# A four-layer graph network: GpSimd forms the bias of the layer norm, the heads' norm's last product gets a place in TensorE's order, and all places are chosen anew

## The chip, the cores and the metric

The kernel runs on one core of one Trainium2 chip. The metric is the device time of one execution in microseconds (us). The kernel before takes 3956.56 us, the median of 3 runs (3955.46 to 3960.7). The profiled execution spans 3957.2 us, with a mean granted TensorE clock of 0.973 of full speed.

A core has five engines with queues of their own: TensorE (PE: matrix products and transposes, with its weight loads PEld beside them), VectorE (DVE), ScalarE (ACT), GpSimd (POOL) and SyncE (SP, which issues the transfers here). They run side by side and wait for each other through semaphores.

## The reference

Thirty-two graphs (B) of 512 nodes (N) with 256 features (D) each go through four layers. Each layer is an attention over the edges of the graph, and is wrapped as `x = layernorm(x + layer(x))`.

```python
# layer 0: 4 heads of 64; e = leaky_relu(e_src + e_dst), masked softmax
out = relu(att @ h + bias) + h
out = (out - out.mean(-1)) / sqrt(out.var(-1) + 1e-6) * gamma + beta   # per head
# layer 1: 1 head; e = relu(f_src + f_dst), masked softmax, then elu
h = x @ W;  out = elu(softmax(where(adj > 0, e, NEG)) @ h)
# layer 2: 8 heads of 32, scaled dot products on adj | adj.T | eye
x1 = layernorm(x + softmax(where(allowed, q @ k.T / sqrt(32), -inf)) @ v @ Wo.T + bo, ln1)
out = layernorm(x1 + relu(x1 @ W1.T + b1) @ W2.T + b2, ln2)
# layer 3: 1 head; e = leaky_relu(f_i + f_j, 0.2), masked softmax
out = softmax(where(adj == 0, NEG, e)) @ (x @ W.T)
```

So a graph has six layer norms over all 256 features (one at the end of each layer, two within layer 2), and one norm per head of 64 in layer 0.

## The kernel before, in words

**Tiling.** The 512 nodes of a graph are four blocks (R = 4) of 128 partitions; a tile such as `y` is 128 x 4 x 256, so a row of the profile with 128x1024 is a whole graph's features. A product goes to one bank of PSUM (512 floats a partition), which `bank` hands out: two banks for layers 0 and 1 (stage "a"), four for the qkv, attention and projection stages ("b"), two for feed forward and layer 3 ("c"). A product must wait until the bank that it is to take has been read. PSUM tiles have the name of what they hold: `o` the products of masked weights with values, `s` the scores, `cp` the context of a head pair transposed, `ctp` its transposition back (and, with input `ctx`, the transposition of the divided context), `wop` the output projection, `f1p` and `f2p` the two products of the feed forward, `gp` a column spread along a row, `h0p`, `h1p`, `h3p` the projections of the layers, `xt1p`, `xt2p`, `xt3p` transpositions of a layer's input, `qkp` and `vp` queries and keys, and values.

**Order.** `graph(b)` is a generator that passes through all stages of one graph: edges, x, layer 0, layer 1, mask, qkv, attention, projection, feed forward, layer 3. Each `yield` in a stage is a cut; `paced` (line 108) turns the i-th cut of stage `name` of graph b into the key `PERIOD * b + PLACES[name][i]`, and `heapq.merge` (line 740) over all 32 generators emits the pieces in the order of their keys. Graphs so overlap as in a pipeline: while one is in its feed forward and layer 3, the next is in attention and the one after in layer 0 and 1. TensorE keeps the emitted order (`tc.manual_schedule` for PE alone, line 739); what the other engines run is ordered by the scheduler of the framework, from the data that each instruction waits for. Keys matter only by their order, so that a finer unit of `PERIOD` does nothing by itself. `in_place` (line 103) ties an instruction of another engine to TensorE's order: it makes the instruction wait for the latest product that was emitted before it. `mask` and `symmetric` use it for the conversion of the edges (line 362) and the union of the two masks (line 381).

**Layer norm** (lines 259 to 280). VectorE takes `bn_stats` and `bn_aggr` of each block of rows (lines 265, 266: mean and variance in `mv`), and forms variance + eps (line 268). GpSimd raises it to the power -0.5 (line 269: 128x4). VectorE multiplies mean, -1 and the power (line 270). ScalarE then computes `y * scale + bias` for the four blocks in place (line 274), where scale is the power and bias that product. `rs` has three rows: variance + eps, power, bias.

**Heads' norm** (lines 282 to 297), used in layer 0. VectorE subtracts the means, ScalarE squares, VectorE sums (line 295 is the sum / 64 + eps), GpSimd raises 128x16 elements to the power -0.5 (line 296), and VectorE multiplies the features by it (line 297). Line 438 (gamma) and 439, and a layer norm follow.

**Around them.** In attention, for each of four head pairs and each of four blocks of keys, TensorE computes the scores, ScalarE their exponentials `pr` (line 549), VectorE multiplies by the mask (line 551, 128x1024, two inputs from SBUF), and `cp` takes four of these as its input; ScalarE copies `cp` to `cs` (line 567). In the projection, VectorE takes reciprocals (line 582) and divides `ctp` into `ctx` (line 586). In layer 1, an `o` product is followed by a reciprocal (line 473, VectorE), relu and exp on ScalarE (474, 475) and two sums on VectorE (476, 478). In the feed forward, ScalarE makes `ft` of `f1p` (line 633), VectorE adds `f2p` (line 647), and lines 649 and 650 follow the second norm. In layer 0, line 398 adds the bias to the values and line 408 scales them (both 128x1024 from SBUF). In layer 3, line 660 is the exponential that `gp` is made from. In layers 0, 1 and 3, line 391 makes the masked weights `pt` (128x512), and line 344 copies `gp` to SBUF.

After all graphs, one flag is read; if a check on edges and sums had failed, a general version would compute everything (it isn't run here).

Of the kernel before, what the change touches and what calls it, by code (L numbers as in the profile page):

```python
# [14 lines left out]
ALU = mybir.AluOpType  # L15
# [7 lines left out]
F32R = mybir.dt.float32r  # L23


PERIOD = 1205
PLACES = {
    "edges": [-226, -113, -5, -1],
    "x": [84],
    "mask": [1464, 1488, 1689, 1689],  # L30
    "layer 0": [
        188, 232, 373, 373, 427, 532, 536, 536, 536, 549, 603, 603, 603, 630, 637, 712, 712, 728,
        758, 758, 766, 779, 787, 791,
    ],
    "layer 1": [1024, 1057, 1078, 1123, 1135, 1135, 1151, 1276, 1299, 1366, 1385],
    "qkv": [1656, 1721, 1771, 1771, 1771, 1849, 1893, 1903, 2016, 2028],
    "attention": [
        1976, 2013, 2122, 2148, 2174, 2174, 2174, 2178, 2178, 2217, 2277, 2277, 2278, 2333, 2363,
        2405, 2452, 2475, 2493, 2527,
    ],  # L40
    "projection": [2590, 2597, 2597, 2606, 2687, 2722, 2820, 2876, 2902, 2949],
    "feed forward": [
        3051, 3062, 3135, 3169, 3169, 3196, 3221, 3327, 3328, 3357, 3381, 3419, 3447, 3483, 3512,
        3560, 3618, 3683,
    ],
    "layer 3": [3958, 3998, 4038, 4074, 4074, 4074, 4082, 4179, 4182, 4185, 4185],
}
STAGES = {"edges": "a", "x": "a", "layer 0": "a", "layer 1": "a", "feed forward": "c", "layer 3": "c"}
ALL = mybir.DependencyInfo(mybir.DependencyClass.Sync, mybir.DependencyReason.DATA)
# [22 lines left out]
def fast_path(ctx: ExitStack, tc: tile.TileContext, a: dict, out: bass.AP, bad: bass.AP):  # L72
# [8 lines left out]
    nc = tc.nc  # L81
    B, N, D = a["x"].shape
    P = 128
    R = N // P
    K = D // P
    H, _, HO = a["w0"].shape
# [13 lines left out]
    def product(what, *args, **kwargs):  # L100
        latest[0] = what(*args, **kwargs).ins.name  # L101

    def in_place(op):

        if latest[0]:
            tc.add_manual_dep(op.ins, latest[0], ALL, reason="in its place")

    def paced(b, name, units):

        i = 0  # L110
        while True:
            stage[0] = STAGES.get(name, "b")
            try:
                next(units)
            except StopIteration as end:
                return end.value
            yield PERIOD * b + PLACES[name][i]
            i += 1
# [124 lines left out]
    def buf(shape, tag, name, bufs, dtype=F32):  # L243

        return sb.tile(shape, dtype, tag=tag + stage[0], name=name, bufs=bufs)

    def bank(name, dtype=F32):
        shape = [P, 2048 // (2 if dtype == BF16 else 4)]
        n = 4 if stage[0] == "b" else 2
        return ps.tile(shape, dtype, tag="mm" + stage[0], name=name, bufs=n)  # L250

    def part(name):

        return buf([P, N], "part", name, {"a": 7, "b": 6, "c": 5}[stage[0]])

    def all_rows(v):
        return v.unsqueeze(1).to_broadcast([P, R, D])

    def layernorm(y, eps):

        st = buf([P, R, 6], "bn", "bn", 2)
        mv = buf([P, R, 2], "mv", "mv", 2)
        rs = buf([P, 3, R], "rs", "rs", 2)
        for r in range(R):
            nc.vector.bn_stats(st[:, r, :], y[:, r, :])  # L265
            nc.vector.bn_aggr(mv[:, r, :], st[:, r, :])
        var = mv[:, :, 1]
        nc.vector.scalar_tensor_tensor(rs[:, 0, :], var, eps, var, op0=ALU.add, op1=ALU.max)  # L268
        nc.gpsimd.tensor_tensor(rs[:, 1, :], rs[:, 0, :], mhalf[:, :R], op=ALU.pow)  # L269
        nc.vector.scalar_tensor_tensor(  # L270
            rs[:, 2, :], mv[:, :, 0], -1.0, rs[:, 1, :], op0=ALU.mult, op1=ALU.mult
        )
        for r in range(R):
            nc.scalar.activation(  # L274
                y[:, r, :],
                y[:, r, :],
                AF.Identity,
                bias=rs[:, 2, r : r + 1],
                scale=rs[:, 1, r : r + 1],
            )  # L280

    def head_layernorm(y, eps):

        G = R * H
        yg = y.rearrange("p r (g d) -> p (r g) d", g=H)
        st = buf([P, 3, G], "lnh", "st", 2)
        nc.vector.tensor_reduce(st[:, 0, :], yg, axis=X, op=ALU.add)
        nc.vector.tensor_scalar_mul(st[:, 0, :], st[:, 0, :], 1.0 / HO)
        nc.vector.tensor_sub(yg, yg, st[:, 0, :].unsqueeze(2).to_broadcast([P, G, HO]))
        for i in range(2):  # L290
            g = slice(i * G // 2, (i + 1) * G // 2)
            sq = part("sq").rearrange("p (g d) -> p g d", d=HO)
            nc.scalar.activation(sq, yg[:, g, :], AF.Square)
            nc.vector.tensor_reduce(st[:, 1, g], sq, axis=X, op=ALU.add)
        nc.vector.tensor_scalar(st[:, 1, :], st[:, 1, :], 1.0 / HO, eps, op0=ALU.mult, op1=ALU.add)  # L295
        nc.gpsimd.tensor_tensor(st[:, 2, :], st[:, 1, :], mhalf[:, :G], op=ALU.pow)  # L296
        nc.vector.tensor_mul(yg, yg, st[:, 2, :].unsqueeze(2).to_broadcast([P, G, HO]))

    def evacuate(i, dst, src):
        if i % 2:  # L300
# [17 lines left out]
    def project(xt, w, cols, name):  # L318

        h = buf([P, R, cols], "h", name, {"a": 2}.get(stage[0], 1))  # L320
        for r in range(R):
            yield
            p = bank(name + "p")
            for k in range(K):
                product(nc.tensor.matmul,
                    p[:, :cols],
                    xt[:, k, r * P : (r + 1) * P],
                    w[:, k, :cols],
                    start=k == 0,
                    stop=k == K - 1,  # L330
                )
            nc.scalar.copy(h[:, r, :], p[:, :cols])
        return h

    def along(cols, name):

        yield
        p = bank("gp")
        for r in range(R):
            product(nc.tensor.transpose,  # L340
                    p[:, r * P : (r + 1) * P], cols[:, r, :].to_broadcast([P, P]), ident
            )
        g = buf([P, N], "gb", name, {"a": 2}.get(stage[0], 1))
        nc.scalar.copy(g, p)  # L344
        return g
# [42 lines left out]
    def kept(name, g, edges, f):  # L388

        t = part(name)  # L390
        nc.vector.scalar_tensor_tensor(t, g, f, edges, op0=ALU.max, op1=ALU.mult)  # L391
        return t


    def layer0(x, xt, at, rd):
        h = yield from project(xt, w0, D + 2 * H, "h0")
        values = hv[:, :, :, :HO]
        nc.vector.tensor_add(
            values,
            h[:, :, :D].rearrange("p r (h e) -> p r h e", h=H),  # L400
            bias0.rearrange("p (h e) -> p h e", h=H).unsqueeze(1).to_broadcast([P, R, H, HO]),
        )
        ex = buf([P, 2, H, R], "ex", "ex0", 2)
        s, d = h[:, :, D : D + H], h[:, :, D + H :]
        nc.scalar.activation(ex[:, 0], s.rearrange("p r h -> p h r"), AF.Exp, scale=-0.99)
        nc.scalar.activation(ex[:, 1], d.rearrange("p r h -> p h r"), AF.Exp, scale=0.99)
        nc.scalar.activation(hv[:, :, :, HO], d, AF.Exp, scale=0.01)
        nc.vector.tensor_mul(values, values, hv[:, :, :, HO:].to_broadcast([P, R, H, HO]))
        y = sb.tile([P, R, D], F32, tag="y", name="y0", bufs=3)
        for hh in range(H):  # L410
            gb = yield from along(ex[:, 0, hh, :].unsqueeze(2), "gb0")
            pt = [kept("pt0", gb, at[:, j, :], ex[:, 1, hh, j : j + 1]) for j in range(R)]
            p = bank("o0")
            o = p[:, : R * HC].rearrange("p (r c) -> p r c", r=R)
            for r in range(R):
                yield
                for j in range(R):
                    product(nc.tensor.matmul,
                    o[:, r, :],
                        pt[j][:, r * P : (r + 1) * P],  # L420
                        hv[:, j, hh, :],
                        start=j == 0,
                        stop=j == R - 1,
                    )
            rdh = rd[:, hh * R : (hh + 1) * R].unsqueeze(2)
            nc.vector.reciprocal(rdh, o[:, :, HO:])
            nc.vector.scalar_tensor_tensor(
                y[:, :, hh * HO : (hh + 1) * HO],
                o[:, :, :HO],
                0.0,  # L430
                rdh.to_broadcast([P, R, HO]),
                op0=ALU.max,
                op1=ALU.mult,
            )
        nc.vector.tensor_add(x, x, all_rows(bet0))
        nc.vector.tensor_add(y, y, h[:, :, :D])
        head_layernorm(y, 1e-6)
        nc.vector.tensor_mul(y, y, all_rows(gam0))
        nc.vector.tensor_add(y, y, x)
        layernorm(y, 1e-5)  # L440
        return y

# [275 lines left out]
    def graph(b):  # L718
        yield PERIOD * b + PLACES["edges"][0]
        rd = sb.tile([P, ND], F32, tag="rd", name="rd", bufs=3)  # L720
# [675 lines left out]
```

## Time and profile before

| what | value |
| --- | --- |
| time, median of 3 | 3956.56 us |
| TensorE busy | 94% of 3957.2 us, 18982 matmuls |
| VectorE busy | 72%, 5626 instructions |
| ScalarE busy | 49%, 4257 instructions |
| GpSimd busy | 9%, 266 instructions |
| power of the layer norm (line 269), 192 times | 1006 to 1991 ns, median 1009 |
| power of the heads' norm (line 296), 32 times | 2914 to 3812 ns, median 3807 |

The profile lists busy time by group of instructions, the waits (idle time of an engine before an instruction, with the instruction that ended the wait as its releaser), a timeline, and the granted TensorE clock. In a timeline row stand the start, the length, the engine, the line, the operation, output and inputs, shapes, how many instructions the row gathers, and in brackets the idle time before it with its releaser. All products of TensorE go through one helper, so they have line 101, and are told apart by the names of their tiles. TensorE's overlapping records make the busy time of a row somewhat longer than its share of the queue. A steady period, from one graph to the next, is a good unit to look at: between the first and the last graphs the same pattern recurs every 117 to 119 us.

### The profile page before, as it was taken

What the parts mean: (1) busy time and instruction counts of PE and PEld (TensorE: products, weight loads), DVE (VectorE), ACT (ScalarE), POOL (GpSimd) and SP (SyncE); (2) the same over time, 40 slices, a digit from 0 to 9 for tenths busy, and PEclk for the clock granted to TensorE, in tenths of its full rate; (3) what the DMA queues carried; (4) which work ended last, traced back from release to release, by engine and by line L of the source; (5) the groups of instructions that cost most, each with busy time, mean ns of one, the idle gap of its engine ahead of it and who ended that gap; (6) DMA issues with size and microseconds to landing.
All of it is one profiled execution on the core that took longest, in us unless ns stands there. A gap on an engine that the chain in (4) does not pass through costs nothing.

```text
span 3957.2 us, 53344 instructions
## 1 busy us (share of the span) xinstructions
PE 3722.2 (94%) x18982; PEld 2832.6 (72%) x18982; DVE 2830.4 (72%) x5626; ACT 1947.7 (49%) x4257; POOL 362.0 (9%) x266
## 2 busy tenths in 40 slices
PE   5899999999999999999999999999999999999996
PEld 4577777777777777777777777777777777777665
DVE  4667777777777777777777777777777777777753
ACT  2444455544455544455554455544455554555442
POOL 0000010010010101010101010101011101011000
PEclk6899999999999999999999999999999999999998
DMA  3222212222222222222222222222222222221110
GB/s 105 75 72 67 70 58 63 70 75 69 68 58 63 70 75 69 68 61 61 69 75 75 62 64 63 64 75 75 62 64 63 65 79 71 62 67 55 52 50 12
DMA packets 180433, 261.20 MB, mean 66 GB/s; under 512 B 36801, under 2 KB 72769, under 8 KB 180161
## 3 DMA queue, kind: packets, MB, share of 16 engines
q1 hardware_dynamic: 180160, 257.71, 23.0%
q8 instruction: 154, 2.52, 0.3%
q14 instruction: 119, 0.97, 0.1%
HBM read 106.57 MB, written 16.78 MB: 31 GB/s over the span
## 4 chain that ended last, share of the span: by engine, by line
PE 51%; DVE 17%; issue 10%; ACT 7%; POOL 7%; SPq 2%; DMA 1%; DVEq 0%; POOLq 0%; ACTq 0%
PE o L101 12%; PE f1p L101 7%; PE f2p L101 6%; DVE pr L551 5%; PE cp L101 4%; POOL rs L269 4%; PE qkp L101 3%; PE h3p L101 3%; POOL st L296 3%; PE wop L101 3%; PE h1p L101 3%; ACT y L274 2%; SPq L510 2%; DVE bn L265 2%; ACT pr L549 2%
## 5 line engine op out<-in xcount | busy, mean ns | idle before, releaser
L551 DVE TENSOR_TENSOR pr<-pr,a 128x1024 f32<-128x1024 f32 x512 | 616.7, 1216 | 220.4 <-ACT pr L549 220.2
L391 DVE SCALAR_TENSOR_TENSOR pt<-gb,ex,at 128x512 f32<-128x512 f32 x768 | 533.3, 743 | 136.3 <-ACT gb L344 136.3
L274 ACT ACTIVATE y<-y,rs 128x256 f32<-128x256 f32 x768 | 397.9, 589 | 386.0 <-DVE rs L270 385.9
L549 ACT ACTIVATE pr<-s 128x512 f32<-128x512 f32 x1024 | 542.3, 615 | 68.7 <-PE s L101 68.3
L101 PE MATMUL cp<-pr,v 128*64 128x512 f32 x2048 | 485.0, 605 | 64.7 <-DVE pr L551 64.7
L101 PEld LDWEIGHTS o<-hv,pt 128*128 128x128 f32 x4096 | 506.1, 198 | 32.6 <-DVE pt L391 16.0
L101 PE MATMUL o<-hv,pt 128*128 128x65 f32 x4096 | 507.2, 280 | 15.4 <-DVE pt L391 11.3
L101 PE MATMUL f2p<-wf,ft 128*128 128x256 f32 x2048 | 492.5, 383 | 23.2 <-ACT ft L633 22.9
L101 PE MATMUL f1p<-yt,wf 128*128 128x256 f32 x2048 | 488.7, 381 | 0.3 <-DVE yt L301 0.3
L101 PE MATMUL o<-h,pt 128*128 128x257 f32 x2048 | 482.5, 383 | 3.2 <-DVE pt L391 3.1
L101 PEld LDWEIGHTS o<-h,pt 128*128 128x128 f32 x2048 | 381.1, 190 | 97.0 <-ACT y L274 23.5
L101 PEld LDWEIGHTS f2p<-wf,ft 128*128 128x128 f32 x2048 | 379.1, 190 | 95.6 <-ACT ft L633 46.8
L633 ACT ACTIVATE ft<-f1p,cols 128x256 f32<-128x256 f32 x512 | 216.7, 479 | 454.5 <-PE f1p L101 454.5
L269 POOL TENSOR_TENSOR rs<-rs,mhalf 128x4 f32<-128x4 f32 x192 | 234.9, 1224 | 2146.4 <-DVE rs L268 2092.5
L101 PEld LDWEIGHTS f1p<-yt,wf 128*128 128x128 f32 x2048 | 382.4, 190 | 52.3 <-issue 0.8
L101 PEld LDWEIGHTS cp<-pr,v 128*64 128x64 f32 x2048 | 127.9, 137 | 346.0 <-DVE pr L551 150.3
L101 PE MATMUL s<-qk 128*128 128x512 f32 x1024 | 359.1, 456 | 1.8 <-ACT pr L549 1.7
L265 DVE BATCH_NORM_STATS2 bn<-y 128x6 f32<-128x256 f32 x768 | 295.8, 409 | 3.5
L101 PEld LDWEIGHTS s<-qk 128*128 128x128 f32 x1024 | 187.0, 190 | 97.9 <-issue 52.7
L101 PE MATMUL qkp<-xt,wqkv 128*128 128x512 f32 x512 | 232.2, 596 | 0.9 <-DVE xt L301 0.9
L296 POOL TENSOR_TENSOR st<-st,mhalf 128x16 f32<-128x16 f32 x32 | 120.9, 3779 | 978.3 <-DVE st L295 978.3
L567 ACT COPY cs<-cp 128x512 f32<-128x512 f32 x128 | 74.5, 582 | 259.6 <-PE cp L101 259.6
(129 smaller groups left out, 4500.0 us busy)
## 6 DMA issues: line engine op xcount, KB each, us to landing
qk<-hi SPq DMA_DIRECT2D x1024, 64.0 KB, 2.0
qk<-lo SPq DMA_DIRECT2D x1024, 64.0 KB, 2.0
adjt<-in_adjt SPq DMA_DIRECT2D x64, 512.0 KB, 3.3
adj<-in_adj SPq DMA_DIRECT2D x64, 512.0 KB, 3.4
xt<-in_xt SPq DMA_DIRECT2D x32, 512.0 KB, 3.6
x<-in_x SPq DMA_DIRECT2D x32, 512.0 KB, 3.6
out<-y SPq DMA_DIRECT2D x32, 512.0 KB, 3.1
wf<-in_w1t SPq DMA_DIRECT2D x1, 1024.0 KB, 7.9
```

Source lines behind the costliest of these rows:

```text
L101: latest[0] = what(*args, **kwargs).ins.name
L265: nc.vector.bn_stats(st[:, r, :], y[:, r, :])
L269: nc.gpsimd.tensor_tensor(rs[:, 1, :], rs[:, 0, :], mhalf[:, :R], op=ALU.pow)
L274: nc.scalar.activation(y[:, r, :], y[:, r, :], AF.Identity, bias=rs[:, 2, r : r + 1], scale=rs[:, 1, r : r + 1],)
L296: nc.gpsimd.tensor_tensor(st[:, 2, :], st[:, 1, :], mhalf[:, :G], op=ALU.pow)
L391: nc.vector.scalar_tensor_tensor(t, g, f, edges, op0=ALU.max, op1=ALU.mult)
L510: nc.sync.dma_start(t[hh // 2][g * DH : (g + 1) * DH, s, hh % 2, :].bitcast(F32), src[hh * DH : (hh + 1) * DH].bitcast(F32),)
L549: nc.scalar.activation(t[:, i, :], s, AF.Exp, scale=QSCALE)
L551: nc.vector.tensor_mul(t, t, edges)
L567: nc.scalar.copy(t, cp)
L633: nc.scalar.activation(ft[:, f, :], p[:, f, :], AF.Relu, bias=bf1[:, ff + f : ff + f + 1])
```

## The change

There are three edits.

1. In the layer norm, the negative mean is formed by VectorE beside the variance, in a fourth row of `rs`, and GpSimd multiplies it by the power right after the power itself. VectorE so has no instruction any more that waits for GpSimd's power; ScalarE's `y` waits for GpSimd's multiply in place of VectorE's.
2. The heads' norm yields before its last product, and this product is `in_place`: it gets a place in the order of the pieces, and waits for the latest product of TensorE. `layer0` passes the cut on with `yield from`, and layer 0 has 25 places in place of 24.
3. The unit of the places is ten times finer (`PERIOD` from 1205 to 12054), and all places are chosen anew.

```diff
-PERIOD = 1205
+PERIOD = 12054
 PLACES = {
-    "edges": [-226, -113, -5, -1],
-    "x": [84],
-    "mask": [1464, 1488, 1689, 1689],
+    "edges": [-1500, -1190, -840, 330],
+    "x": [2350],
+    "mask": [15830, 16030, 17990, 18060],
     "layer 0": [
-        188, 232, 373, 373, 427, 532, 536, 536, 536, 549, 603, 603, 603, 630, 637, 712, 712, 728,
-        758, 758, 766, 779, 787, 791,
+        1454, 3084, 4034, 4734, 5343, 6003, 6003, 6003, 6123, 6123, 6303, 6353, 6653, 6803, 6903,
+        7547, 8047, 8047, 8047, 8047, 8157, 8287, 8339, 8409, 9009,
     ],
-    "layer 1": [1024, 1057, 1078, 1123, 1135, 1135, 1151, 1276, 1299, 1366, 1385],
-    "qkv": [1656, 1721, 1771, 1771, 1771, 1849, 1893, 1903, 2016, 2028],
+    "layer 1": [11207, 11207, 11777, 11777, 11949, 11949, 12013, 13026, 13524, 14085, 15524],
+    "qkv": [17180, 17380, 18240, 18240, 18240, 19020, 19414, 19564, 20945, 21445],
     "attention": [
-        1976, 2013, 2122, 2148, 2174, 2174, 2174, 2178, 2178, 2217, 2277, 2277, 2278, 2333, 2363,
-        2405, 2452, 2475, 2493, 2527,
+        20382, 20382, 20982, 21912, 22162, 22162, 22242, 22280, 22280, 23167, 23307, 23307,
+        24008, 24008, 25003, 25352, 25352, 25442, 25678, 25723,
     ],
-    "projection": [2590, 2597, 2597, 2606, 2687, 2722, 2820, 2876, 2902, 2949],
+    "projection": [26401, 27101, 27301, 27551, 28171, 28651, 29551, 29621, 29621, 30238],
     "feed forward": [
-        3051, 3062, 3135, 3169, 3169, 3196, 3221, 3327, 3328, 3357, 3381, 3419, 3447, 3483, 3512,
-        3560, 3618, 3683,
+        31013, 31150, 31972, 32223, 32223, 32395, 32710, 33801, 33801, 34126, 34314, 34761,
+        35140, 35359, 35915, 36103, 36376, 37329,
     ],
-    "layer 3": [3958, 3998, 4038, 4074, 4074, 4074, 4082, 4179, 4182, 4185, 4185],
+    "layer 3": [39794, 39984, 40896, 41356, 41836, 41836, 41836, 42319, 42349, 42379, 42379],
 }
...
-        rs = buf([P, 3, R], "rs", "rs", 2)
+        rs = buf([P, 4, R], "rs", "rs", 2)
...
         nc.vector.scalar_tensor_tensor(rs[:, 0, :], var, eps, var, op0=ALU.add, op1=ALU.max)
+        nc.vector.tensor_scalar_mul(rs[:, 3, :], mv[:, :, 0], -1.0)
         nc.gpsimd.tensor_tensor(rs[:, 1, :], rs[:, 0, :], mhalf[:, :R], op=ALU.pow)
-        nc.vector.scalar_tensor_tensor(
-            rs[:, 2, :], mv[:, :, 0], -1.0, rs[:, 1, :], op0=ALU.mult, op1=ALU.mult
-        )
+        nc.gpsimd.tensor_tensor(rs[:, 2, :], rs[:, 3, :], rs[:, 1, :], op=ALU.mult)
...
         nc.gpsimd.tensor_tensor(st[:, 2, :], st[:, 1, :], mhalf[:, :G], op=ALU.pow)
-        nc.vector.tensor_mul(yg, yg, st[:, 2, :].unsqueeze(2).to_broadcast([P, G, HO]))
+        yield
+        in_place(nc.vector.tensor_mul(yg, yg, st[:, 2, :].unsqueeze(2).to_broadcast([P, G, HO])))
...
-        head_layernorm(y, 1e-6)
+        yield from head_layernorm(y, 1e-6)
```

In the kernel after the change the power is line 270, GpSimd's multiply line 271, and ScalarE's `y` line 273; the heads' power is line 295, and its last product stays line 297.

## The prediction

> **What bounds the kernel now.** I read first the busy shares, then the waits by engine, then the timeline of one steady period (2040 to 2121 us) on TensorE, VectorE and GpSimd, then the granted clock. From the page:
>
> ```profile
> PE 3722.2 (94%) x18982; PEld 2832.6 (72%) x18982; DVE 2830.4 (72%) x5626; ACT 1947.7 (49%) x4257; POOL 362.0 (9%) x266
> ```
>
> TensorE is the bound: 94% busy. So only what opens or closes a gap on TensorE moves the time. The waits, in us, times, longest:
>
> ```profile
> PE cp L101 <- DVE pr L551: 64.7, 65, 1.9
> PE ctp L101 <- DVE ctx L586: 51.3, 61, 1.7
> PE f2p L101 <- ACT ft L633: 22.9, 39, 3.2
> ...
> DVE rs L270 <- POOL rs L269: 151.2, 164, 1.2
> ...
> DVE y L297 <- POOL st L296: 89.7, 32, 3.1
> ```
>
> VectorE stands 151.2 us at the product (L270) that follows the power, 0.92 each, and 89.7 us at the heads' norm's last product (L297). TensorE's two largest waits are for VectorE. TensorE in the steady period (start, length, last the wait):
>
> ```profile
> 2047.01 1.08 PE L101 MATMUL cp<-pr,v 128*64 128x512 f32 x4 [0.84 <-DVE pr L551]
> ...
> 2057.51 1.08 PE L101 MATMUL cp<-pr,v 128*64 128x512 f32 x4 [1.11 <-DVE pr L551]
> ...
> 2096.24 0.33 PE L101 MATMUL ctp<-ident,ctx 128*128 128x128 f32 x1 [0.26 <-DVE ctx L586]
> 2098.01 1.16 PE L101 MATMUL ctp<-ident,ctx 128*128 128x128 f32 x5 [1.44 <-DVE ctx L586]
> ```
>
> With 0.49 at f2p (2041.44) these are all of the period's waits: 4.14 us. VectorE around them:
>
> ```profile
> 2044.59 1.22 DVE L297 TENSOR_TENSOR y<-y,st 128x1024 f32<-128x1024 f32 x1 [2.79 <-POOL st L296]
> ...
> 2054.07 1.19 DVE L551 TENSOR_TENSOR pr<-pr,a 128x1024 f32<-128x1024 f32 x1
> 2056.16 0.16 DVE L270 SCALAR_TENSOR_TENSOR rs<-mv,rs 128x4 f32<-128x4 f32 x1 [0.90 <-POOL rs L269]
> ...
> 2095.01 0.16 DVE L270 SCALAR_TENSOR_TENSOR rs<-mv,rs 128x4 f32<-128x4 f32 x1 [0.77 <-POOL rs L269]
> ```
>
> L297's 2.79 ends in the first cp wait, L270's 0.90 stands ahead of the last mask product of the second, and L270's 0.77 and the sums queued behind it stand ahead of the ctx products. Last, the clock (us, busy of PE, PEld, DVE, ACT, POOL, granted clock, DMA share, GB/s):
>
> ```profile
> 2094.82:2098.24 3.42, 1.72 (x9) 1.11 (x9) 3.19 (x12) 2.61 (x6) 0.16 (x1) 1.00 0.00 0
> 2098.24:2101.65 3.41, 3.41 (x14) 3.00 (x13) 2.30 (x6) 2.17 (x5) 1.01 (x1) 0.50 0.21 76
> ```
>
> After a window in which TensorE idled 1.70 of 3.42 us the clock is 0.50 for a window; windows idle for up to 1.45 were not followed by that. From graph to graph the starts of L296 are 118.9 us apart with such a window and 117.2 without; 16 of 27 steady periods had one. So it costs 1.7 us, 1.0 a period on average.
>
> **What the skill says.** (1) The Trainium skill, "SBUF — State Buffer", section "SBUF: two separate sides": VectorE and GpSimd share a pair of ports, exclusively locked; a VectorE instruction with two SBUF inputs, or a GpSimd one that reads SBUF, holds it for its whole length and the other blocks. The trace agrees for one direction:
>
> ```profile
> 2054.14 1.99 POOL L269 TENSOR_TENSOR rs<-rs,mhalf 128x4 f32<-128x4 f32 x1 [9.58 <-DVE rs L268]
> ...
> 2098.32 1.01 POOL L269 TENSOR_TENSOR rs<-rs,mhalf 128x4 f32<-128x4 f32 x1 [3.35 <-DVE rs L268]
> ```
>
> The power took 1.99 when L551 had started 0.07 us before it, and 1.01 otherwise. Not for the other: L381 started at 2098.38, inside the second power, and took its usual 1.22. The measurement decides: VectorE delays GpSimd, not the reverse. (2) "TensorE: Matmul & The Clock Gate", "Part 1: The HAM clock gate": after an idle window of about 3.4 us the clock halves, and the windows run freely. The 0.50 above agrees in length; here half a window idle was enough. (3) "GPSIMD Engine Reference", "3.1 Elementwise — side-by-side cycle accounting": about 2.6 cycles an element beside the dispatch.
>
> **The change, part by part.**
>
> (a) GpSimd multiplies. Removed: one L270 per norm, 192 of 0.16 us, and its waits of 151.2 us. Added on VectorE: a scalar multiply of 128x4, about 0.16 as L268's row shows (0.15), of which 0.08 from start to start. VectorE's work stays equal; the fourth row of rs costs nothing, as its two buffers stay. Added on GpSimd: a multiply of 4 elements. No row shows it. Below: the two power shapes, 128x4 at 1.01 and 128x16 at 3.81, give 0.233 an element and an intercept of 0.08; a memset of 128x4 takes 0.10. Page (3) leaves the elements at some hundredths, an estimate. Above: as dear as the power, 1.0. I take 0.12, as the power's price lies in its elements. Hand-over GpSimd to ScalarE replaces VectorE to ScalarE (2056.16+0.16 to 2056.35), at nothing. ScalarE's y (L274) therefore starts about as before: power 1.0, then 0.12 for 0.16. What was queued behind L270 on VectorE, up to 0.9 us a norm, comes earlier. But a VectorE that doesn't wait issues its next large product at once, and by (1) that holds up power, multiply, or both. Before, only the power could be hit (1.99 with L551; 1.92 at 104.35 us with L398, 1.36 with L391 at 2119.63), since VectorE was idle when L270's turn came. Now each may lose up to 1.0 to 1.2.
>
> (b) The heads' norm. L297 gets a place and a wait for the latest product. In the compiled order of both kernels it stands at the same point of VectorE, between the third and fourth mask product of a head pair, and the product it waits for is a v projection placed well before. It still waits for the power of 128x16. I cost it at nothing, and 2.79 and the 0.84 after it stay.
>
> (c) The places, from the compiled order. A block of f1p (8 of 1.89 us) now stands ahead of the second cp's last products: that takes the 1.11. Ahead of the ctx transposes stand now o, eight xt3p and h0p, some 3 us: that takes 0.26 and 1.44. The ft pair comes 0.4 earlier against f2p: 0.13 is left of 0.49. The new order also brings consumers nearer to their sources. Walking the steady period by hand with the measured lengths:
> - s after a pr: 0.1; first ctp after its cs copy (L567): 0.3.
> - the fourth o of layer 1 now stands after two ctp and two h0p blocks. It needs the bank that ScalarE's exp (L475) of the one before last frees; that waits for a reciprocal (L473) behind the feed forward's L649, L476, L650 and L478 on VectorE: 1.2 with y (L274) of the norm held up 1.0 by L551, 0.2 without.
> - xt3p after the rows of y: 0.7.
> - gp of layer 3 needs L660, which stands on ScalarE behind the four y of layer 1's norm (2.07), and these behind power and multiply. L398 holds the power 1.0 and L408 the multiply 0.7: 1.7; without contention about 0.
>
> Sum after: 0.84 + 0.13 + 0.1 + 0.3 + 1.2 + 0.7 + 1.7 = 4.97 against 4.14, so +0.83 a period. The gap before gp is again 1.7 us long, so I leave the clock dips as frequent as before. 27 steady periods: +22.4 us; fill and drain as before. 3956.6 + 22.4 = **3979 us**.
>
> **Rivals.**
> - **A, faster: little contention.** 1.7 and 1.0 of the waits above vanish: 2.27 - 4.14 = -1.87 a period, -50; with half of the clock dips gone (0.5 x 27 = 13) 3893, with all 3879. For it: L381 and the power lay side by side, and if the power starts first it may have read its inputs already. Against: 1.99 and 1.92 in just the norms that matter.
> - **B, faster: no new wait at all.** 0.97 left and no dips: -3.17 - 1.0 = -4.17 a period, 3844. For it: the walk assumes each source as late as before, though VectorE has 0.9 us a norm in hand. Against: VectorE's work stays and is only shifted.
> - **C, slower: dear multiply, or GpSimd starved.** With 1.0 for the multiply, the two chains through y (o and gp) each gain 0.9: +2.6 a period, +71, 4028; with a dip in each period (0.7 x 27 = 19) 4047. For it: the power is dear, and nothing here shows a multiply. Against: the memset's 0.10.
> - **D, no change.** The forecast's waits, but spread so that fewer windows idle for 1.7: -0.8 a period cancels +0.83: 3957.
>
> **How the numbers follow.** Forecast 0.41, A 0.28, B 0.07, C 0.13, D 0.11. Faster is A and B: 0.35; same is D: 0.11; slower the forecast and C: 0.54. The range goes from A with all dips gone, 3880, to just above C without dips, 4035; outside lie B and C's upper half with the tails, about 0.17.
>
> **What would show it.** Multiply at about 0.12 when alone: (a) right; about 1.0: C. Power or multiply of 1.3 to 2.2 whenever L551, L398 or L408 started just before: contention; nearly all powers at 1.0: A. L297 still waiting about 2.8: (b). TensorE's waits: cp from 65 times to about 32, ctp for ctx near nothing; new ones at o for exp, xt3p for y, gp for ex. Clock dips: where, and in how many periods. The forecast fails if VectorE, free of its wait, has its reciprocals and sums out so early that o and gp find their inputs ready.

## The result and the profile after

The changed kernel takes 4049.03 us (median of 4, 4046.61 to 4053.68) against 3957.48 before: a ratio of 1.0232, 95% interval 1.0217 to 1.0246. It is 92 us slower; 3979 was forecast. A steady period, from one power of the heads' norm (now line 295) to the next, is 120.4 us, or 123.7 in the 9 of 25 periods that have a clock dip. Before it was 117.2, or 118.9 in 17 of the same 25. That is 121.6 against 118.4 on average: 3.2 us a period, 81 us over these 25 periods. The rest of the 92 is spent before them (2 us) and after them (8 us).

First a line of the page with the busy time of each engine, then the waits of TensorE (in us, how many, the longest):

```profile
PE 3789.4 (94%) x18982; PEld 2842.0 (70%) x18982; DVE 2803.7 (69%) x5626; ACT 1943.7 (48%) x4257; POOL 524.4 (13%) x458
```

```profile
PE gp L101 <- ACT ex L660: 50.4, 32, 1.7
PE o L101 <- ACT exp L475: 33.6, 28, 1.2
PE xt1p L101 <- ACT y L273: 30.6, 63, 20.0
PE cp L101 <- DVE pr L551: 27.1, 35, 2.3
PE f2p L101 <- ACT ft L633: 26.6, 38, 3.5
PE xt3p L101 <- ACT y L273: 25.1, 35, 12.2
```

The wait for ctx (51.3 before) is gone, that at cp has halved (64.7 to 27.1). New are the waits at gp, o, xt3p and xt1p, and all four end on ScalarE: on y itself (line 273) or on something that stood behind y in ScalarE's queue. (The long single waits of 20.0 at xt1p and 12.2 at xt3p belong to the first graphs; the kernel before has them too, 19.7 and 12.0.) So y is late. GpSimd's timeline shows why; the two rows from 2026 us are the norm at the end of layer 1, those from 2099 us the norm at the end of layer 0:

```profile
2026.44 1.99 POOL L270 TENSOR_TENSOR rs<-rs,mhalf 128x4 f32<-128x4 f32 x1 [7.93 <-DVE rs L269]
2028.51 0.91 POOL L271 TENSOR_TENSOR rs<-rs 128x4 f32<-128x4 f32 x1
...
2099.20 3.13 POOL L270 TENSOR_TENSOR rs<-rs,mhalf 128x4 f32<-128x4 f32 x1 [9.58 <-DVE rs L269]
2102.41 0.64 POOL L271 TENSOR_TENSOR rs<-rs 128x4 f32<-128x4 f32 x1
```

A power that is left alone takes 1.01 us, the multiply 0.20: 98 of 192 powers and 99 multiplies do. The others take longer, while VectorE runs a large product: 63 powers take 1.9 to 2.0, and 31, about one a graph, 3.1. This is called held below. VectorE's timeline beside the power at 2099.20:

```profile
2098.97 0.15 DVE L268 SCALAR_TENSOR_TENSOR rs<-mv 128x4 f32<-128x4 f32 x1
2099.04 0.16 DVE L269 TENSOR_SCALAR rs<-mv 128x4 f32<-128x4 f32 x1
2099.11 2.35 DVE L551 TENSOR_TENSOR pr<-pr,a 128x1024 f32<-128x1024 f32 x2
...
2101.78 1.21 DVE L594 TENSOR_TENSOR y<-y,bo_b 128x1024 f32<-128x1024 f32 x1
```

Two mask products of line 551 run from 2099.11 to 2101.46 without a gap, and the power, which starts 0.09 us after the first, ends 0.87 after the second. The multiply, at 2102.41, then starts inside the addition of line 594 and takes 0.64. In the kernel before, the product of mean and power (2056.16 in the prediction's lines) stood between the two mask products, and VectorE waited there; the second came only behind it:

```profile
2056.24 1.22 DVE L551 TENSOR_TENSOR pr<-pr,a 128x1024 f32<-128x1024 f32 x1
```

In the changed kernel there follows on TensorE:

```profile
2104.72 0.33 PE L101 MATMUL xt1p<-ident,y 128*128 128x128 f32 x1 [0.16 <-ACT y L273]
2105.22 0.77 PE L101 MATMUL xt1p<-ident,y 128*128 128x128 f32 x5 [0.16 <-ACT y L273]
2106.61 1.99 PE L101 MATMUL f2p<-wf,ft 128*128 128x256 f32 x8 [0.63 <-ACT ft L633]
```

The four blocks of y come one by one, and f2p waits for `ft` (line 633), which stands on ScalarE behind them. The clock, in windows of the same profile (columns as in the prediction):

```profile
2030.28:2033.70 3.42, 1.75 (x15) 1.35 (x13) 3.20 (x6) 2.82 (x9) 0.00 (x0) 1.00 0.00 0
2033.70:2037.11 3.41, 3.41 (x19) 3.41 (x19) 2.75 (x5) 0.00 (x0) 0.00 (x0) 0.50 0.00 0
2037.11:2040.53 3.42, 3.42 (x18) 3.42 (x18) 1.23 (x1) 0.00 (x0) 0.00 (x0) 0.50 0.24 87
```

After the gap before gp (1.67 us, ending at 2032.35) the clock is at half for two windows, where the kernel before had one. Such a dip costs 3.3 us: a period with it takes 123.7 us, one without 120.4.

### The profile page after: what moved, and what is told of

It is laid out like the page before. It is cut to its first block, busy times and chain, and to the rows that moved or that the text cites. A ratio compares the mean times of both kernels' runs of the same rounds, so it can differ in the third digit from the quotient of the medians.

```text
span 4048.4 us, 53476 instructions
## 1 busy us (share of the span) xinstructions
PE 3789.4 (94%) x18982; PEld 2842.0 (70%) x18982; DVE 2803.7 (69%) x5626; ACT 1943.7 (48%) x4257; POOL 524.4 (13%) x458
## 4 chain that ended last, share of the span: by engine, by line
PE 56%; DVE 20%; ACT 10%; POOL 9%; issue 2%; SPq 2%; DMA 1%; DVEq 0%; POOLq 0%; ACTq 0%
PE o L101 17%; PE f1p L101 10%; PE f2p L101 9%; ACT y L273 7%; PE cp L101 5%; POOL rs L270 4%; DVE pr L551 4%; PE qkp L101 3%; PE s L101 3%; POOL st L295 3%; PE h1p L101 3%; DVE bn L265 2%; DVE pt L391 2%; POOL rs L271 2%; PE gp L101 2%
## 5 line engine op out<-in xcount | busy, mean ns | idle before, releaser
L270 POOL TENSOR_TENSOR rs<-rs,mhalf 128x4 f32<-128x4 f32 x192 | 321.0, 1672 | 2132.0 <-DVE rs L269 2096.2
L101 PEld LDWEIGHTS o<-hv,pt 128*128 128x128 f32 x4096 | 530.6, 205 | 40.2 <-DVE pt L391 19.7
L101 PE MATMUL o<-hv,pt 128*128 128x65 f32 x4096 | 533.1, 287 | 22.1 <-DVE pt L391 18.8
L101 PE MATMUL o<-h,pt 128*128 128x257 f32 x2048 | 490.8, 387 | 38.8 <-ACT exp L475 33.6
L101 PE MATMUL cp<-pr,v 128*64 128x512 f32 x2048 | 478.9, 603 | 27.2 <-DVE pr L551 27.1
L344 ACT COPY gb<-gp 128x512 f32<-128x512 f32 x192 | 111.9, 583 | 301.3 <-PE gp L101 297.4
```

## The experiments

Theory H: GpSimd's power and multiply are held by VectorE's large products with two inputs that started just before, so y comes late, and TensorE waits for what hangs on y. Rivals: O, the new places put consumers too near, whatever GpSimd does; M, GpSimd's multiply and its hand-over are dear in themselves; W, the new wait of the heads' product costs. Line numbers shift by a few in kernels with added lines. All ratios are to the kernel before, on the same chip.

**1. The parts of the change, one by one.** First the changed kernel with the layer norm's edit undone:

```diff
-        nc.vector.tensor_scalar_mul(rs[:, 3, :], mv[:, :, 0], -1.0)
...
-        nc.gpsimd.tensor_tensor(rs[:, 2, :], rs[:, 3, :], rs[:, 1, :], op=ALU.mult)
+        nc.vector.scalar_tensor_tensor(
+            rs[:, 2, :], mv[:, :, 0], -1.0, rs[:, 1, :], op0=ALU.mult, op1=ALU.mult
+        )
```

> The changed kernel with the product of mean and power back on VectorE (its line as before), the new places and the placed last product of the heads' norm kept. TensorE's order is that of the changed kernel. Theory H (GpSimd held up): the power and the multiply wait for VectorE's products with two inputs, above all in layer 0's norm, where two of line 551 now stand back to back (power 3.13 us, multiply 0.64); with VectorE waiting for the power there, its products come after it, y starts some 2.4 us earlier in layer 0 and 0.7 in layer 1, TensorE's waits at xt1p, at the f2p after it and at half of gp go: about -2.3 us a period, 3985 us (3965 to 4005). Rival O (the new order alone: consumers placed too near to their sources): within 15 us of the changed kernel, 4035 or more.

Measured: 3930.98 us, ratio 0.9931 (0.9916 to 0.9946). It is faster than both kernels, and is called the 3931 us kernel below. So the multiply on GpSimd costs 118 us in the new order, and the rest of the change gains 26: O is wrong, and H has the sign right but not the size (3965 to 4005 expected). There is no clock dip in 25 steady periods, which take 117.3 to 117.7 us. Of the new waits, xt1p, o and half of gp are gone:

```profile
PE gp L101 <- ACT ex L661: 25.4, 32, 0.8
```

Then the layer norm's edit alone, in the kernel before (the first diff of the change, with the old places):

> The kernel before with only the layer norm's edit (negative mean on VectorE, multiply on GpSimd); old places, heads' norm as before, TensorE's order that of the kernel before. Theory H: layer 0's power is again held by two products of line 551 (about 3.1 us), so xt1p waits about 1 us more, but the wait at cp that VectorE's wait caused (1.11) goes, and part of the ctx wait (0.77 of VectorE's own): about the kernel before, 3940 to 3975 us. Theory O: the same or faster than before, 3900 to 3957. Rival M (the multiply on GpSimd and its hand-over are dear wherever they stand): 4010 or more.

Measured: 4102.84 us, 1.0369 (1.0353 to 1.0385), +145 us (the 4103 us kernel below). This is in M's range alone, and yet the trace doesn't show what M says: 127 of 192 multiplies take 0.2 us, the others at most 1.0, and ScalarE's y starts 0.03 us after the multiply's end. Nor does it show what H expected: five of 192 powers take 1.9 us or more, and a single one 3.1. So what is shown below of the holding is shown for the new order; part 4 takes up the old one.

The third edit alone (the cut and the wait at line 297, place 850), in the kernel before:

> The kernel before with only the third edit: the yield and the wait for the latest product at the heads' norm's last product, with a 25th place (850) in layer 0. All engines' orders are those of the kernel before. Both theories: 3957 us, within 0.2%. Rival W (the added wait itself costs, since VectorE's queue stands behind it): slower by 0.3% or more, with line 297 waiting for a product of TensorE.

Measured: 3956.85 us, 0.9996 (0.9988 to 1.0005): nothing. And the new places alone, without that edit:

> The kernel before with the new places alone (the 25th place of layer 0 unused): no cut and no wait at the heads' norm, product of mean and power on VectorE. All engines' orders are those of the 3931 us kernel. Both theories: 3931 us within 0.2%. Rival W (the wait of the placed product helps or hurts in the new order): outside 3923 to 3939.

Measured: 3931.8 us, 0.993 (0.9913 to 0.9947). W is wrong in both orders. The sum, in the new order: places -26, heads' product 0, GpSimd's multiply +118.

**2. Is it the holding?** The changed kernel, with a wait added to VectorE, where the kernel before had one:

```diff
         nc.gpsimd.tensor_tensor(rs[:, 2, :], rs[:, 3, :], rs[:, 1, :], op=ALU.mult)
+        nc.vector.tensor_copy(rs[:, 3, :], rs[:, 2, :])
```

> The changed kernel with one VectorE copy of 128x4 added to each layer norm, that reads what GpSimd's multiply wrote; it stands behind one large product on VectorE and makes VectorE wait for GpSimd as the kernel before did. All else in every engine's order is as in the changed kernel. Theory H: no multiply is held any more (0.20 everywhere), a power by one product at most (1.99, not 3.13); y of layer 0's norm comes 1.6 us earlier and that of layer 1's 0.7, so an added wait makes the kernel faster: 4010 us (3985 to 4030). Rival O: the order is the same and VectorE loses about 1 us a norm, so 4049 or more.

Measured: 3956.08 us, 0.9999 (0.9991 to 1.0008), better than the range. A pure addition, a useless copy before which VectorE waits 1.1 us on average, takes 93 us off the changed kernel. GpSimd's timeline at the end of layer 0, and VectorE's copy:

```profile
1934.05 1.99 POOL L270 TENSOR_TENSOR rs<-rs,mhalf 128x4 f32<-128x4 f32 x1 [9.58 <-DVE rs L269]
1936.12 0.20 POOL L271 TENSOR_TENSOR rs<-rs 128x4 f32<-128x4 f32 x1
```

```profile
1936.35 0.17 DVE L272 COPY rs<-rs 128x4 f32<-128x4 f32 x1 [1.18 <-POOL rs L271]
1936.43 1.22 DVE L552 TENSOR_TENSOR pr<-pr,a 128x1024 f32<-128x1024 f32 x1
```

The second product now stands behind the copy; 3.13 + 0.64 has become 1.99 + 0.20.

The other way, without any wait: VectorE is only delayed by some 0.3 us, so that the power starts first.

```diff
         nc.vector.tensor_scalar_mul(rs[:, 3, :], mv[:, :, 0], -1.0)
+        for i in range(4):
+            nc.vector.tensor_scalar_mul(sp[:, i, :], mv[:, :, 0], 1.0)
```

> The changed kernel with four VectorE multiplies of 128x4 (one SBUF input, into scratch that nothing reads) behind the negative mean in each layer norm. They wait for nothing and take some 0.3 us together, so that GpSimd's power starts before VectorE's next large product instead of just after it. Orders of TensorE and VectorE otherwise as in the changed kernel. Theory H (GpSimd is held by a product that started before it): every power takes 1.01 us, none 2.0 or 3.1; the multiply behind it is still held by the product then running; y comes 0.7 to 1.2 us earlier in three norms of a period, though VectorE has 0.3 us more to do in each: 3993 us (3960 to 4020). Rival N (holding is no cause; VectorE's order and load are): 4049 or more.

Measured: 3954.08 us, 0.9994 (0.9985 to 1.0003), 95 us off, beyond the range on the good side. Every one of the 192 powers takes 1.01 to 1.04 us. GpSimd, VectorE and, from another graph, ScalarE ahead of gp: the first two show the feed forward's second norm, the third the end of layer 1:

```profile
2083.36 1.01 POOL L273 TENSOR_TENSOR rs<-rs,mhalf 128x4 f32<-128x4 f32 x1 [14.96 <-DVE rs L270]
2084.45 0.39 POOL L274 TENSOR_TENSOR rs<-rs 128x4 f32<-128x4 f32 x1
```

```profile
2083.57 1.21 DVE L554 TENSOR_TENSOR pr<-pr,a 128x1024 f32<-128x1024 f32 x1
```

```profile
1514.27 0.37 ACT L335 COPY h<-h3p 128x258 f32<-128x258 f32 x1 [0.44 <-PE h3p L101]
```

The power has a start of 0.21 us and runs its 1.01 beside the product, which takes its usual 1.21; the multiply, which starts inside the product, is held 0.19. In layer 0's norm VectorE's order also changed (one product, not two, follows the small ones), so these 95 us are not of the delay alone; part 3 takes the norms one by one. And gp still waits 0.7 us here. ScalarE is done with y early enough to stand 0.44 us for TensorE's own h3p, so this rest of the wait comes from how near gp is placed to h3p, not from the norm. This kernel and the one with the copy still take 23 to 25 us more than the 3931 us kernel; that is the most that is left, in this order, for M and for the waits of the added instructions together.

The same delay in the 3931 us kernel, where the product of mean and power is on VectorE. Four small multiplies:

> The kernel with new places, placed heads' product and the product of mean and power on VectorE (3931 us), with the same four small multiplies before the power's wait; in VectorE's order the product of mean and power then follows them at once, ahead of the large product. Theory H: every power 1.01 us (62 of 192 took 1.9), y in the feed forward's second norm and in layer 1's some 0.9 us earlier, gp's wait of 0.8 gone: 3910 us (3895 to 3925). Rival: VectorE stands 1.0 us in each norm with its large product behind it, which costs more than y gains: 3931 or more, with more waits at cp.

Measured: 4010.72 us, 1.0139 (1.0122 to 1.0156). The rival is right: the powers are all 1.01 to 1.04, gp's wait is 0.7 where none was expected, and 80 us are lost to the 3931 us kernel, where cp waited 46.6 us in all. The mask products now stand behind VectorE's wait of 0.8 us:

```profile
PE cp L101 <- DVE pr L555: 112.1, 94, 2.6
```

And three:

> The kernel with new places, placed heads' product and the product of mean and power on VectorE (3931 us), with three small VectorE multiplies ahead of the power's wait (four put that wait ahead of the large product; with three the large product stands ahead of it again). Theory H: every power starts just before the large product and takes 1.01, VectorE runs the large product meanwhile and waits hardly at all; y comes 0.8 us earlier in the feed forward's second norm and layer 1's: 3908 us (3890 to 3922). Rival: three small instructions a norm on VectorE, or y at an earlier time, displace other work of VectorE and ScalarE: 3931 or more.

Measured: 3940.47 us, 0.9954 (0.9937 to 0.997). Missed, and the timelines of GpSimd and VectorE say why:

```profile
1960.37 2.07 POOL L272 TENSOR_TENSOR rs<-rs,mhalf 128x4 f32<-128x4 f32 x1 [15.00 <-DVE rs L269]
```

```profile
1960.36 1.22 DVE L555 TENSOR_TENSOR pr<-pr,a 128x1024 f32<-128x1024 f32 x1
```

The product started 0.01 us before the power, and that was enough to hold it for its whole length: 92 powers take 2.1. So in this kernel more powers were held, not fewer; it leaves open what a delay just long enough would have brought here.

**3. Which norm, and how much.** `layernorm` got a switch, and the product of mean and power went back to VectorE in one norm of the changed kernel: at the end of layer 0, or at the end of layer 1.

```diff
-        layernorm(y, 1e-5)
+        layernorm(y, 1e-5, dve=True)
```

> The changed kernel with the product of mean and power back on VectorE in the norm at the end of layer 0 alone; GpSimd multiplies in the five others. In VectorE's order it stands between two products of line 551, so the power there is held by one of them (about 2.0 us, not 3.1) and no multiply is. Theory H, with its largest part in this norm: y 1.7 us earlier, TensorE's waits of 0.9 at xt1p and 0.8 at the f2p behind it go, those at o (1.3) and gp (1.8) stay: -1.6 a period, 4003 us (3975 to 4015; the low end if the clock dips go too). Rival (the held powers of the other norms make the difference): 4035 or more.

Measured: 3994.66 us, 1.0091 (1.0074 to 1.0108): 54 us off. The power there is held by one product (1.92 us), as expected, and no longer by two. xt1p waits no more, the f2p behind it neither; gp and o stay as they were, and so do nearly all dips (8 of the 25 periods), with periods of 118.6 and 121.9, so the gain is 1.8 us a period.

> The changed kernel with the product of mean and power back on VectorE in the norm at the end of layer 1 alone. All orders are as in the changed kernel, but for this product behind line 398. Theory H: the power there is still held by line 398 (2.0 us), the multiply no more by line 408 (0.9): y 0.7 us earlier, the wait at gp falls from 1.8 to about 1.0: -0.8 a period, 4026 us (4000 to 4035; the low end if the gap is now too short for the clock dips). Rival: 4045 or more.

Measured: 3992.73 us, 1.0084 (1.0068 to 1.0101): 56 us off, more than twice what was expected, from one instruction of 0.16 us a graph that went back to VectorE. gp waits 0.8 in place of 1.7, and there is no dip any more in any steady period: 119.5 or 119.8 in all. The wait is 0.9 a period (some 26 us), the dips (9 of 3.3 us) are the other half. TensorE's waits at gp, here:

```profile
PE gp L101 <- ACT ex L666: 25.4, 32, 0.8
```

The two norms together make up 110 of the 118 us. The small rest is a balance, not a sign that the other norms are free. TensorE's instructions stand in the same order in the changed and the 3931 us kernel, so their starts can be laid side by side. In a period without a dip the changed kernel loses 1.8 us at xt1p and f2p, 0.9 at gp and 1.5 at o, whose exp stands behind the feed forward's second norm; it gains 0.8 at the second cp, since VectorE no longer waits there, and 0.4 at xt3p.

**4. Two ways on, that failed.** In the 3931 us kernel, gp of layer 3 is placed later, and layer 3's first o behind the queries and keys:

```diff
-    "layer 3": [39794, 39984, 40896, 41356, 41836, 41836, 41836, 42319, 42349, 42379, 42379],
+    "layer 3": [39794, 39984, 40896, 41356, 41836, 41836, 42166, 42349, 42349, 42379, 42379],
```

> The kernel with new places, placed heads' product and the product of mean and power on VectorE (3931 us), with layer 3's gp placed some 2.6 us of TensorE's work later (41836 to 42166) and its first o3 after the queries and keys (42319 to 42349). Theory of nearness (gp waits since it is placed right behind the h3 products, while ScalarE copies these behind four y): the wait of 0.8 to 0.95 us a period at gp goes: 3906 us (3895 to 3920). Rival: the wait only moves to the next instruction that needs ScalarE or VectorE: 3925 to 3940.

Measured: 3993.58 us, 1.0096 (1.0079 to 1.0113). The wait at gp is gone (2.1 us in all), and 63 us are lost: o waits 41.3 us in 135 places for the masked weights (line 392 there), qkp 25 us for the transposed input. The wait at gp was replaced by larger ones.

The old places with GpSimd's multiply (4103 us) have their largest wait at h0p, 106.3 us, for an exp of ScalarE that frees a bank. On VectorE the scheduler had put the product with layer 2's gamma, which reads y, ahead of the reciprocal that this exp needs; VectorE stands at it 3.3 us a graph, waiting for y. The experiment ties that product behind the reciprocal:

```diff
-        nc.vector.tensor_mul(y, y, all_rows(ln2g))
+        yield
+        in_place(nc.vector.tensor_mul(y, y, all_rows(ln2g)))
```

> The kernel with the old places and GpSimd's multiply (4103 us), with one thing more: the product with layer 2's gamma after the second norm of the feed forward (the first instruction of VectorE that reads y) gets a cut at place 3777 and waits for the product of TensorE placed there, so that in VectorE's order it stands behind the sums and the reciprocal of layer 1 instead of ahead of them. TensorE's order is the same. Theory S (the scheduler put VectorE's reader of y ahead of the reciprocal that frees a bank for TensorE, and VectorE stood 3.3 us at it): the waits of 4.0 us a period at h0p and the clock dip in each period go: 3955 us (3925 to 3990). Rival H alone (GpSimd held by VectorE's products is what makes that kernel slow): powers and multiplies are held as before, 4070 or more.

Measured: 4142.41 us, 1.0468 (1.0451 to 1.0486), slower still. The waits of TensorE, of the 4103 us kernel and then of this one:

```profile
PE h0p L101 <- ACT exp L474: 106.3, 58, 2.1
```

```profile
PE ctp L101 <- DVE ctx L585: 92.8, 93, 1.9
```

The wait at h0p went as expected, and one of nearly the same size came at ctx, with two dips a period where the 4103 us kernel has one (periods of 123 and 126 us). So the cause of the 145 us in the old places stays open: the order that the scheduler gave VectorE is part of it, but mending it at one point moved the wait.

## Why the prediction was wrong

The direction was right, the size was not: +22 us forecast, +92 measured, outside the range of 3880 to 4035 us. By its steps:

- **What bounds the kernel**: right. Only gaps of TensorE and the clock count; the third edit opens no gap on TensorE and changed nothing by itself.
- **(a), the price**: right. The multiply takes 0.20 us (0.12 taken, 0.1 to 1.0 bounded), the power 1.01. VectorE's waits for the power are gone.
- **(b)**: right. Line 297 waits 89.6 us in all, as before (89.7), and the edit alone is worth nothing in either order.
- **(c), what it removes**: right. ctx and the second cp wait are gone, the first cp wait is 0.71 (0.84).
- **(c), what it brings**: the waits that were walked through came out close. From start to next start on TensorE, beyond the usual, averaged over 25 steady periods: gp 1.83 (1.7), o 1.31 (1.2), xt3p 0.64 (0.7), f2p 0.26 (0.13). At gp part of this was luck: the forecast put all 1.7 on the held power and multiply and "about 0" on the rest, but with no power held gp still waits 0.7, for TensorE's own h3p.
- **The step that failed** is a term that the sum does not have: the norm at the end of layer 0. The power was held there by two products of line 551 in a row (3.13 us) and the multiply by the addition of line 594 (0.64); y came some 2.5 us later than with 1.01 and 0.20, and xt1p (0.91) and the f2p behind it (0.80) waited. That is 1.7 us a period; putting this norm back gave 1.8, 54 us. The text said that VectorE "issues its next large product at once" and let the power lose "up to 1.0 to 1.2", one product, and then applied this to two norms of three. With the 1.7 the same sum gives +2.5 a period, +68 us. Where the other 24 us come from stays open; they are 0.7 us a period, with the first and last graphs, which the forecast left as before.
- **The clock**: "as frequent as before" was wrong in count and in cost, and by luck the two errors nearly cancelled: 9 of 25 periods at 3.3 us for 17 of 25 at 1.7 (the forecast's 16 of 27 was a little low). But the dips were counted as a background, and in the new order they hang on the gap at gp: with that gap at 0.8 there is none.
- **Split by cause**, the forecast put +73 us on the holding (2.7 a period) and -51 on the rest; measured are +118 for GpSimd's multiply and -26 for the places. The two splits don't divide the change in the same way: the +118 already has in it what VectorE's freed waits give back, and in the 3931 us kernel 64 powers take 1.8 us or more too. So the missing term is better read from its own experiment, 54 us.
- **Rivals**: C gave 4047, the time that came, with "dear multiply, or GpSimd starved". Its first half is wrong (0.20), its second half is what happened; but the sum was built on the first, so that its number came by luck. A's argument, that a power which starts first is not held, is right (the small multiplies show it); in the changed kernel it starts second in half of the norms.

## What to carry to other kernels

Taking a wait off an engine that is not the bound brings forward what that engine does next, and here these next products held the very chain (power, multiply, y) whose end TensorE waits for. So ask of a removed wait what will start in its place and what that shares with the chain; here the length of what started next, taken twice where two stood in a row, was the price to put in. Where a small instruction of GpSimd is on the path, look at the VectorE row that started just before it: a power that started 0.01 us after a product of 1.22 us took 2.07 us, one with a lead of 0.21 us took its usual 1.01.

## What the runs showed of the hardware

- The holding goes one way for these instructions. In the kernel with the delay (3954 us), 62 mask products (line 554) started while a power was running, and they took 1.21 us (1.210 to 1.215); their median over all 512 is 1.219 in the kernel before and 1.217 there. The Trainium skill, "SBUF — State Buffer", section "SBUF: two separate sides", has whichever starts first block the other for its whole length; the traces show that for VectorE's products (2.07 us for a power that started 0.01 us after one) and not for GpSimd's power.
- A held instruction gets in some 0.15 us before the recorded end of the product that holds it (2083.57 + 1.21 = 2084.78; the multiply of 0.20 ended at 2084.84), but two products back to back let nothing in between (3.13 us).
- Not every instruction of VectorE holds a power: in the changed kernel 30 powers started inside a division of line 586, which reads `ctp` from PSUM and had some 0.33 us to go, and took 1.01 us.
- A clock dip lasted one window of 3.41 us (before) or two (6.83, after), and the ones shown came after a window in which TensorE was idle for half of it (1.70 and 1.67 us). But the idle time alone doesn't decide it. In the kernel before, the windows from 1739.84 and from 1978.78 us were idle for 1.70 and 1.69, and only the first was followed by a dip; in the 4103 us kernel the one from 1061.30 was idle for 1.83 and none followed; in the kernel with the later gp the one from 1647.26 was idle for 0.67 and one followed. So "half a window idle was enough" is true of some windows, and what decides stays open.
